# The last product of a gap in a pair of the maxima's PSUM banks, and the values in two halves: one change to an attention-and-experts block

## The chip, the cores and the metric

The kernel runs on one core of a Trainium2 chip. The metric is the device time of one execution in microseconds. The kernel before takes 2642.56 us, the median of three runs (2640.65 to 2642.76). The execution that the profiler recorded took 2650.03 us, and its trace spans 2648.3 us from the first to the last instruction.

## The reference

The input x has 32 sequences of 512 tokens with 256 features, in float32. Two causal attentions with 16 heads of 16 features follow each other. What the kernel calls a = 0 is ordinary attention with x itself as values; a = 1 has the same queries, other keys, and as values what the first attention got wrong.

```python
qk = x @ W_attn + b_attn                 # q and k
y  = causal_attn(q, k, v=x)
e  = x[:, 1:] - y[:, :-1]
k2 = x[:, :-1] @ W_k2 + b_k2
y2 = causal_attn(q[:, 1:], k2, e)        # one row of zeros ahead
x  = layernorm(x + proj(y) + proj(y2))
x  = layernorm(x + experts(x))           # 8 experts, top 2, summed by token
```

The experts' part has 512 tokens, those of the first sequence; for the 31 other sequences the second norm follows the first directly. Shapes and types of all results stay as they are in the kernel before.

## The kernel before, in words

**Groups and steps.** Four heads make a group, four groups a sequence, so there are 128 groups. `step(n)` (line 654) is called once for each n and works on several groups at once: the maxima of the scores of group n, the scores and exponentials of group n-1 (a = 0, and of n-2 for a = 1), the values of group n-2 and the normalization of n-2 and n-3.

**Slots and gaps.** A step has five slots (`slot`, line 393; the shapes are in `units`, line 263, and `banks`, line 345), and behind each slot a gap, filled from the list `rest[s]`. In a slot TensorE computes two things for a pair of heads at a time: the maxima's products (`sm`, lines 286 and 301), which VectorE reduces to a largest value per query (`top`, line 325), and the scores' products (`sc`, line 365), which ScalarE turns into exponentials (`pt`, line 382); GpSimd then cuts the diagonal block (line 386). Pair 1 of the scores comes first, then pair 0 of the maxima, then pair 1 of the maxima interleaved with pair 0 of the scores. In slots 0 and 3 each pair of maxima has two reductions, 768 and 256 columns wide; in the other slots it has one of 1024 columns.

**What fills the gaps.** In most steps: behind slot 0 the transposed maxima (`mt`, line 338) and then a half projection (`pj`, line 223, odd n) or an output projection (`po`, line 526, even n); behind slot 1 the values for a = 0 (`av`, line 434); behind slot 2 a transposition (`yt`, line 449) and a projection (`pj`); behind slot 3 `yt` and then `pj` or `po`; behind slot 4 the values for a = 1, in every fourth step with two transpositions `ys` (line 515) behind them. In the steps 12 to 20 the experts' products (`gu`, `dn`) stand ahead of these. A filling is one accumulation in one PSUM bank, and ScalarE or VectorE then copies it out. In `values` the four heads' products write four different strips of 32 partitions of one bank, four blocks of keys after each other, and one copy of 512 columns (line 442) takes them out.

**PSUM.** Its eight banks are in two pools. `bank` (line 79) hands out one bank of four: the scores' four products of a slot use them all, and so does every filling. `pair_of_banks` (line 76) hands out two neighbouring banks, and there are two such pairs: the maxima of a slot's pair 0 take one, those of pair 1 the other. A pool hands out what has been free longest, so the banks go round in turn, and a tile's first product waits until the last reader of the bank's previous tile is done.

**Order.** TensorE and SyncE run in the order of the code (`manual_schedule`, line 67); the order of the other engines is made by a scheduler. TensorE issues in order: a product that waits holds up those behind it.

Of the kernel before, what the change touches and what calls it, by code (L numbers as in the profile page):

```python
# [39 lines left out]
def block_kernel(  # L40
# [35 lines left out]
    def pair_of_banks(name):  # L76
        return psum.tile([P, NH2, T], F32, tag="two", name=name, bufs=2)

    def bank(name):
        return psum.tile([P, T], F32, tag="one", name=name, bufs=4)  # L80


# [246 lines left out]
    def halve(n):  # L329
        t, top = mx[n % 2], groups[n]["top"]  # L330
        nc.vector.tensor_copy(half(t[:, :, :, 0:2]), top)
        nc.vector.tensor_sub(half(t[:, :, :, 2:4]), top, t[:, :, :, 0:2])

    def augment(n):
        d = groups[n]
        ps = bank(f"mt{n}")
        for i in range(NB):
            nc.tensor.transpose(ps[:, i * P : (i + 1) * P], mx[n % 2][:, i].rearrange("p h s -> p (h s)"), ident)  # L338
        d["m"] = grp.tile([P, T], F32, tag="m", name=f"m{n}")
        nc.scalar.copy(half(d["m"]), ps)  # L340
# [82 lines left out]
            if after:  # L423
                after()

    def values(n, a):
        b, g = divmod(n, NG)
        d = groups[n]
        vals = (v_pad, e_pad)[a]
        ps = bank(f"av{n}_{a}")  # L430
        order = [0, 2, 1, 3] if a == 0 else [0, 1, 3, 2]
        for j in order:
            for h in range(GH):
                nc.tensor.matmul(  # L434
                    ps[HS * h : HS * (h + 1), j * P :],
                    vals[:, j, (g * GH + h) * HV : (g * GH + h) * HV + HS],
                    d["pt", a, j, h // NH2][:, h % NH2],
                    start=(j == order[0]),
                    stop=(j == order[-1]),
                )  # L440
        avs = d["avs", a] = work.tile([P, T], F32, tag="avs", name=f"avs{n}_{a}")
        nc.scalar.copy(avs, ps)  # L442

    def normalize(n, a):
        b, g = divmod(n, NG)
# [52 lines left out]
    def load_residual(b):  # L498
        s = seqs[b]
        s["xr"] = seq.tile([P, NB, C], F32, tag="xr", name=f"xr{b}", bufs=1)  # L500
        nc.sync.dma_start(s["xr"], x[b].rearrange("(n p) c -> p n c", p=P))

    def biased(b, part):

        two = slice(2 * part, 2 * part + 2)
        t = seqs[b]["xr"]
        nc.gpsimd.tensor_add(t[:, two], t[:, two], bp2.unsqueeze(1).to_broadcast([P, 2, C]))

    def turn(b):
        s = seqs[b]  # L510
        ysT = s["ysT"] = work.tile([P, NC, T], F32, tag="ysT", name=f"ysT{b}", bufs=1)
        for c in range(NC):
            ps = bank(f"ys{b}_{c}")
            for i in range(NB):
                nc.tensor.transpose(ps[:, i * P : (i + 1) * P], s["y"][:, i, c * P : (c + 1) * P], ident)  # L515
            nc.scalar.copy(ysT[:, c], ps)

    def attended(b, i):

# [50 lines left out]

        nc.vector.tensor_scalar(wt, wt, 0.5, None, ALU.mult)

    def biases():
        acc = moe["acc"] = seqs[0]["h"]
        for k in range(NB * C // T):
            ps = bank(f"bd{k}")
            for i in range(2 * k, 2 * k + 2):
                nc.tensor.matmul(
                    ps[:, (i % 2) * C : (i % 2 + 1) * C], moe["wT"][0:E, i * P : (i + 1) * P], moe["b_dn"],
                    start=True, stop=True,  # L580
                )
            two = slice(2 * k, 2 * k + 2)
            nc.vector.tensor_add(acc[:, two], ps.rearrange("p (i c) -> p i c", c=C), acc[:, two])

    def turn_tokens():
        moe["xT"] = const.tile([P, NC, T], F32, name="x1T")
        for c in range(NC):
            ps = bank(f"x1T{c}")
            for i in range(NB):
                nc.tensor.transpose(ps[:, i * P : (i + 1) * P], seqs[0]["h"][:, i, c * P : (c + 1) * P], ident)  # L590
            nc.vector.tensor_copy(moe["xT"][:, c], ps)

    def load_hidden(e):
        gu = moe["gu", e] = seq.tile([P, NC, 2, NF * P], F32, tag="gu", name=f"gu{e}", bufs=1)
# [27 lines left out]
            nc.vector.tensor_scalar(t, t, -LIMIT, 1.0, ALU.max, ALU.add)  # L622
            nc.gpsimd.tensor_mul(moe["h", e][:, f], moe["sig"], t)

    def down(e):
        for k in range(NB * C // T):
            ps = bank(f"dn{e}_{k}")
            for i in range(2 * k, 2 * k + 2):
                for f in range(NF):
                    nc.tensor.matmul(  # L630
                        ps[:, (i % 2) * C : (i % 2 + 1) * C],
                        moe["h", e][:, f, i * P : (i + 1) * P],
                        moe["dn", e][:, f],
                        start=(f == 0),
                        stop=(f == NF - 1),
                    )
            for i in range(2 * k, 2 * k + 2):
                nc.vector.scalar_tensor_tensor(
                    moe["acc"][:, i],
                    ps[:, (i % 2) * C : (i % 2 + 1) * C],  # L640
                    moe["w"][:, i, e : e + 1],
                    moe["acc"][:, i],
                    ALU.mult,
                    ALU.add,
                )

# [7 lines left out]
    def step(n):  # L654
        ready = lambda k: 0 <= k < n_all
        rest = [[] for _ in units]
        b, r = divmod(n, NG)
        if r == 1 and b + 1 < B:
            load(b + 1)
        if r == 3 and b + 1 < B:  # L660
            load_next(b + 1)
        if ready(n):
            prepare(n)
        if ready(n - 3):
            rest[3].append(lambda: normalize(n - 3, 1))
        if ready(n):
            rest[4].append(lambda: halve(n))
        if ready(n - 1):
            rest[0].append(lambda: augment(n - 1))
        if ready(n - 2):  # L670
            soon = n > n_all
            rest[0 if soon else 1].append(lambda: values(n - 2, 0))
            rest[1 if soon else 2].append(lambda: normalize(n - 2, 0))
            rest[4].append(lambda: values(n - 2, 1))
        two = n // 2 + 1
        if ready(2 * two):
            if n % 2 == 0:
                rest[2].append(lambda: project(two, 1))
                rest[4].append(lambda: spread(two, 1))
            else:  # L680
                rest[2] += [lambda: project(two, 0), lambda: spread(two, 0)]
                rest[0].append(lambda: project(two, 2, 0, T // 2))
                rest[3] += [lambda: project(two, 2, T // 2), lambda: spread(two, 2)]
        b, r = divmod(n - 3, NG)
        if r == NG - 1 and 0 <= b < B:
            rest[4].append(lambda b=b: turn(b))

        for b in range(B):
            end = (b + 1) * NG - 1
            last = b == B - 1  # L690
            for part in range(2):
                if n == (end + 4 if last else min(end + 5 + 2 * part, n_all)):
                    for i in range(2 * part, 2 * part + 2):
                        rest[0 if last or i % 2 == 0 else 3].append(lambda b=b, i=i: attended(b, i))
                if n == (end + 3 if last else end + 4):
                    rest[1 + 2 * part].append(lambda b=b, part=part: biased(b, part))
            if n == (end + 2 if last else end + 3):
                rest[3].append(lambda b=b: load_residual(b))
            if 0 < b < B - 1 and n == end + 8:
                rest[1].append(lambda b=b: store(b))  # L700


        e = n - first_expert
        if e == -1:
            rest[4] += [route, turn_tokens, lambda: load_hidden(0), lambda: load_down(0)]
        if e == 0:
            rest[0].insert(0, biases)
        if 0 <= e < E:
            rest[3].insert(0, lambda: hidden(e, 0, 0))
            rest[4].insert(0, lambda: hidden(e, 0, 1))  # L710
        if 0 <= e - 1 < E:
            rest[0].insert(0, lambda: hidden(e - 1, 1, 0))
            rest[1].insert(0, lambda: hidden(e - 1, 1, 1))
            rest[2].insert(0, lambda: down(e - 1))
            if e < E:
                rest[1].append(lambda: load_hidden(e))
                rest[2].append(lambda: load_down(e))
        if e == E:
            rest[4].append(lambda: second_norm(0, moe["acc"]))
        for s in range(len(units)):  # L720
            slot(n, s)
            for f in rest[s]:
                f()

    for m in range(3):
        project(0, m)
# [91 lines left out]
```

## Time and profile before

| | before |
|---|---|
| median of three runs | 2642.56 us (2640.65 to 2642.76) |
| the profiled execution | 2650.03 us |
| its span in the trace | 2648.3 us |
| mean granted TensorE clock | 0.989 |
| VectorE busy | 1943.7 us (73%) |
| ScalarE busy | 1757.0 us (66%) |
| GpSimd busy | 1724.0 us (65%) |
| TensorE matmul records | 33,808 |
| copies of the values, line 442 | 256 of 587 ns |

How to read it: busy is the time in which an engine executes at least one instruction. TensorE has two rows in the profile, PE for products and PEld for loads of the stationary operand. The ends of products are modelled, so the distance from one product's start to the next one's tells more than their durations. The 1.7 us between the profiled execution's time and its span lie before the first and after the last instruction. From slot 0 to the next step's slot 0 most steps of the trace take 19.1 us, and every fourth, that with the `ys`, 20.1 us.

### The profile page before, as it was taken

The numbers are of one execution on the slowest core, as the hardware profiler recorded it, in microseconds if no ns is written. First come the engines' busy times: TensorE is split into PE (matmuls) and PEld (weight loads), VectorE is DVE, ScalarE is ACT, GpSimd is POOL, SyncE is SP. The second block draws the span as 40 slices with busy tenths as digits, with TensorE's granted clock in tenths as the row PEclk, the third lists the DMA queues.
The fourth block names the chain that finished last, engine by engine and source line by source line (L and its number), as shares of the span: only waits on it lengthen the run. The fifth ranks groups of instructions, "written<-read, shape, count | busy, mean of one in ns | idle before, by whom it ended". The sixth has DMA issues, their size and how long they took to land.

```text
span 2648.3 us, 82677 instructions
## 1 busy us (share of the span) xinstructions
PE 2569.7 (97%) x33808; PEld 1742.7 (66%) x33808; DVE 1943.7 (73%) x3225; ACT 1757.0 (66%) x3416; POOL 1724.0 (65%) x3318
## 2 busy tenths in 40 slices
PE   6999999999999999999999999999999999999997
PEld 3666666666666666666666666666666666666665
DVE  5777777677777777777777777777777777777773
ACT  2666554467777767776767777676777767677774
POOL 4555555567666676766667666666766666676664
PEclk7999999999999999999999999999999999999998
DMA  5233233233334343333433333343333334233320
GB/s 136 69 89 89 73 85 91 79 81 97 89 75 104 83 104 82 95 90 74 105 81 99 88 91 93 75 105 81 90 96 90 94 76 104 82 90 96 88 67 25
DMA packets 167402, 231.91 MB, mean 88 GB/s; under 512 B 21624, under 2 KB 91248, under 8 KB 167024
## 3 DMA queue, kind: packets, MB, share of 16 engines
q1 hardware_dynamic: 164592, 226.17, 33.1%
q8 instruction: 269, 4.41, 0.7%
q14 instruction: 109, 0.89, 0.1%
q10 hardware_dynamic: 2368, 0.42, 0.1%
q0 software_dynamic: 64, 0.02, 0.0%
HBM read 75.41 MB, written 16.78 MB: 35 GB/s over the span
## 4 chain that ended last, share of the span: by engine, by line
PE 91%; ACT 3%; issue 2%; POOL 2%; DVE 2%; DMA 1%; SPq 0%; ACTq 0%; POOLq 0%; DVEq 0%
PE sc L365 28%; PE av L434 22%; PE pj L223 13%; PE sm L301 10%; PE yt L449 6%; PE po L526 4%; PE mt L338 3%; ACT pt L382 2%; PE gu L607 2%; PE ys L515 1%; PE dn L630 1%; DVE top L325 1%; PE sm L286 1%; POOL pk L241 0%; DMA bp_qk<-in_b_qkk 0%
## 5 line engine op out<-in xcount | busy, mean ns | idle before, releaser
L325 DVE TENSOR_REDUCE top<-sm 128x2 f32<-128x768 f32 (+3 forms) x1800 | 1536.3, 907 | 589.0 <-PE sc L365 328.7
L382 ACT ACTIVATE pt<-sc 128x512 f32<-128x512 f32 (+1 forms) x2564 | 1323.3, 602 | 322.9 <-PE sc L365 315.9
L386 POOL TENSOR_SCALAR_AFFINE_SELECT pt<-pt 128x256 f32<-128x256 f32 x2048 | 787.7, 407 | 531.1 <-ACT pt L382 530.3
L301 PE MATMUL sm<-kk_t,q_t 32*128 32x512 f32 (+2 forms) x7168 | 1034.8, 381 | 18.7 <-DVE top L325 9.0
L365 PE MATMUL sc<-q_t,kk_t 32*128 32x256 f32 (+3 forms) x8192 | 1045.5, 338 | 3.4 <-DVE h L529 2.0
L365 PEld LDWEIGHTS sc<-q_t,kk_t 32*128 32x128 f32 x8192 | 701.2, 184 | 260.4 <-issue 160.2
L365 PE MATMUL sc<-m,minus 32*128 32x256 f32 (+3 forms) x4096 | 756.4, 318 | 0.0
L301 PEld LDWEIGHTS sm<-kk_t,q_t 32*128 32x128 f32 x7168 | 613.8, 190 | 25.2 <-DVE top L325 11.7
L365 PEld LDWEIGHTS sc<-m,minus 32*128 32x128 f32 x4096 | 507.1, 185 | 10.0
L223 PE MATMUL pj<-xT,wq_sb 128*128 128x256 f32 (+1 forms) x1020 | 400.3, 516 | 8.5 <-DVE wq_sb L112 8.5
L442 ACT COPY avs<-av 128x512 f32<-128x512 f32 x256 | 150.2, 587 | 325.9 <-PE av L434 325.9
L286 PE MATMUL sm<-hide,pick 32*128 32x256 bf16 (+1 forms) x2560 | 339.2, 258 | 0.0
L434 PE MATMUL av<-pt,e_pad 128*32 128x512 f32 (+3 forms) x4096 | 304.2, 437 | 17.9 <-ACT pt L382 13.3
L434 PE MATMUL av<-pt,v_pad 128*32 128x512 f32 (+3 forms) x4096 | 304.4, 437 | 14.6 <-POOL pt L386 4.2
L235 ACT ACTIVATE pk<-pj,bp_qk 128x256 f32<-128x256 f32 (+1 forms) x255 | 151.2, 593 | 194.7 <-PE pj L223 185.4
L241 POOL TENSOR_TENSOR pk<-pk,lead 128x512 fp32r<-128x512 f32 x192 | 244.7, 1274 | 15.7 <-ACT lead L240 5.0
L434 PEld LDWEIGHTS av<-pt,v_pad 128*32 128x32 f32 x4096 | 136.8, 110 | 170.3 <-issue 128.4
L223 PEld LDWEIGHTS pj<-xT,wq_sb 128*128 128x128 f32 x1020 | 176.1, 192 | 96.1 <-issue 65.1
L434 PEld LDWEIGHTS av<-pt,e_pad 128*32 128x32 f32 x4096 | 130.9, 110 | 152.8 <-issue 148.0
L478 POOL TENSOR_TENSOR y<-y,y 128x256 f32<-128x256 f32 x128 | 96.4, 753 | 118.7 <-DVE mv L542 68.2
L449 PE MATMUL yt<-ident,avs 128*128 128x128 f32 x1024 | 168.0, 287 | 2.1 <-ACT pt L382 0.9
L449 PEld LDWEIGHTS yt<-ident,avs 128*128 128x128 f32 x1024 | 109.2, 141 | 75.3 <-ACT pt L382 70.3
(90 smaller groups left out, 1980.5 us busy)
## 6 DMA issues: line engine op xcount, KB each, us to landing
q_t<-lead SPq DMA_DIRECT2D x256, 128.0 KB
q_t<-pk SPq DMA_DIRECT2D x256, 128.0 KB
kk_t<-lead SPq DMA_DIRECT2D x256, 128.0 KB
kk_t<-pk SPq DMA_DIRECT2D x256, 128.0 KB
xT<-in_xT SPq DMA_DIRECT2D x32, 512.0 KB
x<-in_x SPq DMA_DIRECT2D x32, 512.0 KB
xr<-in_x SPq DMA_DIRECT2D x32, 512.0 KB
out<-h SPq DMA_DIRECT2D x31, 512.0 KB
```

The source lines that it names most:

```text
L223: nc.tensor.matmul(ps[:, 0 : hi - lo], wq_sb[:, m, c, part * P : (part + 1) * P], seqs[b]["xT"][:, c, lo:hi], start=(c == 0), stop=(c == N ...
L235: nc.scalar.activation(pk[:, lo:hi], ps[:, 0 : hi - lo], AF.Identity, bias=bp_qk[:, m, part : part + 1])
L241: nc.gpsimd.tensor_sub(half(pk), pk, lead)
L286: nc.tensor.matmul(ps[hh][:, 0 if alone else hh].rearrange("p (k c) -> p k c", c=P)[:, first::step], pick[rows], hide[rows, kinds[0] : kin ...
L301: nc.tensor.matmul(part(ps[hh], i, na, at)[:, 0 if alone else hh], half(d["q"][rows, k, i * P : (i + 1) * P]), half(d["kk"][rows, a : a + ...
L325: nc.vector.tensor_reduce(to, view, AX.X, ALU.max)
L365: nc.tensor.matmul(ps[hh][:, at * P : at * P + T - j * P], half(keys), half(queries[:, j * P :]), start=(k == 0), stop=(k == 2),)
L382: nc.scalar.activation(pt[:, hh, lo:hi], ps[hh][:, lo:hi], AF.Exp, scale=HD**-0.5)
L386: nc.gpsimd.affine_select(diag, diag, pattern=[[0, NH2], [1, P]], compare_op=ALU.is_ge, fill=0.0, base=-a, channel_multiplier=-1,)
L434: nc.tensor.matmul(ps[HS * h : HS * (h + 1), j * P :], vals[:, j, (g * GH + h) * HV : (g * GH + h) * HV + HS], d["pt", a, j, h // NH2][:, ...
L442: nc.scalar.copy(avs, ps)
L449: nc.tensor.transpose(ps[:, i * P : (i + 1) * P], d["avs", a][:, i * P : (i + 1) * P], ident)
```

## The change

A flag says that a filling is the last in its gap that uses a bank. While it is set, `bank` hands out the first bank of a pair from the maxima's pool in place of one of the four. So that every entry of a gap's list uses exactly one bank, functions that used several are called once for each: the values in two halves of 256 queries, `turn`, `biases`, `turn_tokens` and `down` once for each bank that they fill. The lists are written in another way but come out in the same order; an entry is now marked as one that fills a bank (`do`) or one that does not (`also`).

```diff
+    last_of_gap = [False]
+
     def bank(name):
+        if last_of_gap[0]:
+            return pair_of_banks(name)[:, 0]
         return psum.tile([P, T], F32, tag="one", name=name, bufs=4)
...
-    def values(n, a):
+    def values(n, a, lo, hi):
...
-        ps = bank(f"av{n}_{a}")
-        order = [0, 2, 1, 3] if a == 0 else [0, 1, 3, 2]
+        ps = bank(f"av{n}_{a}_{lo}")
+        order = [j for j in ([0, 2, 1, 3] if a == 0 else [0, 1, 3, 2]) if j * P < hi]
         for j in order:
+            at = max(lo, j * P)
             for h in range(GH):
                 nc.tensor.matmul(
-                    ps[HS * h : HS * (h + 1), j * P :],
+                    ps[HS * h : HS * (h + 1), at - lo : hi - lo],
                     vals[:, j, (g * GH + h) * HV : (g * GH + h) * HV + HS],
-                    d["pt", a, j, h // NH2][:, h % NH2],
+                    d["pt", a, j, h // NH2][:, h % NH2, at - j * P : hi - j * P],
...
-        avs = d["avs", a] = work.tile([P, T], F32, tag="avs", name=f"avs{n}_{a}")
-        nc.scalar.copy(avs, ps)
+        if lo == 0:
+            d["avs", a] = work.tile([P, T], F32, tag="avs", name=f"avs{n}_{a}")
+        nc.scalar.copy(d["avs", a][:, lo:hi], ps[:, 0 : hi - lo])
...
-            rest[0 if soon else 1].append(lambda: values(n - 2, 0))
-            rest[1 if soon else 2].append(lambda: normalize(n - 2, 0))
-            rest[4].append(lambda: values(n - 2, 1))
+            for lo, hi in ((0, T // 2), (T // 2, T)):
+                do(0 if soon else 1, values, n - 2, 0, lo, hi)
+            do(1 if soon else 2, normalize, n - 2, 0)
+            for lo, hi in ((0, T // 2), (T // 2, T)):
+                do(4, values, n - 2, 1, lo, hi)
...
         for s in range(len(units)):
             slot(n, s)
-            for f in rest[s]:
+            filling = [k for k, (_, fills) in enumerate(rest[s]) if fills]
+            for k, (f, _) in enumerate(rest[s]):
+                last_of_gap[0] = k == filling[-1] if filling else False
                 f()
+            last_of_gap[0] = False
```

In the built kernel the instructions of SyncE, VectorE and GpSimd are the same and in the same order as before. ScalarE has 256 copies more, each pair of half copies where the whole one stood. TensorE has the products in the same order, with the values' split: 24 in place of 16 for each of 256 values.

More of the change, by code (lines that the diff above doesn't have):

```diff
@@ L507, in biased, with turn @@
         nc.gpsimd.tensor_add(t[:, two], t[:, two], bp2.unsqueeze(1).to_broadcast([P, 2, C]))
-    def turn(b):
+    def turn(b, c):
         s = seqs[b]
[L511 to L516, printed above, removed]
+        if c == 0:
+            s["ysT"] = work.tile([P, NC, T], F32, tag="ysT", name=f"ysT{b}", bufs=1)
+        ps = bank(f"ys{b}_{c}")
+        for i in range(NB):
+            nc.tensor.transpose(ps[:, i * P : (i + 1) * P], s["y"][:, i, c * P : (c + 1) * P], ident)
+        nc.scalar.copy(s["ysT"][:, c], ps)
     def attended(b, i):
@@ L571, in route, with biases, turn_tokens @@
         nc.vector.tensor_scalar(wt, wt, 0.5, None, ALU.mult)
-    def biases():
+    def biases(k):
         acc = moe["acc"] = seqs[0]["h"]
[L575 to L591, printed above, removed]
+        ps = bank(f"bd{k}")
+        for i in range(2 * k, 2 * k + 2):
+            nc.tensor.matmul(
+                ps[:, (i % 2) * C : (i % 2 + 1) * C], moe["wT"][0:E, i * P : (i + 1) * P], moe["b_dn"],
+                start=True, stop=True,
+            )
+        two = slice(2 * k, 2 * k + 2)
+        nc.vector.tensor_add(acc[:, two], ps.rearrange("p (i c) -> p i c", c=C), acc[:, two])
+    def turn_tokens(c):
+        if c == 0:
+            moe["xT"] = const.tile([P, NC, T], F32, name="x1T")
+        ps = bank(f"x1T{c}")
+        for i in range(NB):
+            nc.tensor.transpose(ps[:, i * P : (i + 1) * P], seqs[0]["h"][:, i, c * P : (c + 1) * P], ident)
+        nc.vector.tensor_copy(moe["xT"][:, c], ps)
     def load_hidden(e):
@@ L623, in hidden, with down @@
             nc.gpsimd.tensor_mul(moe["h", e][:, f], moe["sig"], t)
[L625 to L639, printed above, removed]
+    def down(e, k):
+        ps = bank(f"dn{e}_{k}")
+        for i in range(2 * k, 2 * k + 2):
+            for f in range(NF):
+                nc.tensor.matmul(
                     ps[:, (i % 2) * C : (i % 2 + 1) * C],
[L641 to L644, printed above, removed]
-                )
+                    moe["h", e][:, f, i * P : (i + 1) * P],
+                    moe["dn", e][:, f],
+                    start=(f == 0),
+                    stop=(f == NF - 1),
+                )
+        for i in range(2 * k, 2 * k + 2):
+            nc.vector.scalar_tensor_tensor(
+                moe["acc"][:, i],
+                ps[:, (i % 2) * C : (i % 2 + 1) * C],
+                moe["w"][:, i, e : e + 1],
+                moe["acc"][:, i],
+                ALU.mult,
+                ALU.add,
+            )
     n_all = B * NG
@@ L663, in step @@
             prepare(n)
+        do = lambda gap, f, *args: rest[gap].append((partial(f, *args), True))
+        also = lambda gap, f, *args: rest[gap].append((partial(f, *args), False))
+        e = n - first_expert
+        if e == 0:
+            for k in range(NB * C // T):
+                do(0, biases, k)
+        if 0 <= e - 1 < E:
+            do(0, hidden, e - 1, 1, 0)
+            do(1, hidden, e - 1, 1, 1)
+            for k in range(NB * C // T):
+                do(2, down, e - 1, k)
+        if 0 <= e < E:
+            do(3, hidden, e, 0, 0)
+            do(4, hidden, e, 0, 1)
         if ready(n - 3):
-            rest[3].append(lambda: normalize(n - 3, 1))
+            do(3, normalize, n - 3, 1)
         if ready(n):
-            rest[4].append(lambda: halve(n))
+            also(4, halve, n)
         if ready(n - 1):
-            rest[0].append(lambda: augment(n - 1))
+            do(0, augment, n - 1)
         if ready(n - 2):
             soon = n > n_all
-            rest[0 if soon else 1].append(lambda: values(n - 2, 0))
-            rest[1 if soon else 2].append(lambda: normalize(n - 2, 0))
-            rest[4].append(lambda: values(n - 2, 1))
+            for lo, hi in ((0, T // 2), (T // 2, T)):
[3 more added lines that the diff above has]
+                do(4, values, n - 2, 1, lo, hi)
         two = n // 2 + 1
@@ L677, in step @@
             if n % 2 == 0:
-                rest[2].append(lambda: project(two, 1))
-                rest[4].append(lambda: spread(two, 1))
-            else:
-                rest[2] += [lambda: project(two, 0), lambda: spread(two, 0)]
-                rest[0].append(lambda: project(two, 2, 0, T // 2))
-                rest[3] += [lambda: project(two, 2, T // 2), lambda: spread(two, 2)]
+                do(2, project, two, 1)
+                also(4, spread, two, 1)
+            else:
+                do(2, project, two, 0)
+                also(2, spread, two, 0)
+                do(0, project, two, 2, 0, T // 2)
+                do(3, project, two, 2, T // 2)
+                also(3, spread, two, 2)
         b, r = divmod(n - 3, NG)
         if r == NG - 1 and 0 <= b < B:
-            rest[4].append(lambda b=b: turn(b))
+            for c in range(NC):
+                do(4, turn, b, c)
         for b in range(B):
@@ L693, in step @@
                     for i in range(2 * part, 2 * part + 2):
-                        rest[0 if last or i % 2 == 0 else 3].append(lambda b=b, i=i: attended(b, i))
+                        do(0 if last or i % 2 == 0 else 3, attended, b, i)
                 if n == (end + 3 if last else end + 4):
-                    rest[1 + 2 * part].append(lambda b=b, part=part: biased(b, part))
+                    also(1 + 2 * part, biased, b, part)
             if n == (end + 2 if last else end + 3):
-                rest[3].append(lambda b=b: load_residual(b))
+                also(3, load_residual, b)
             if 0 < b < B - 1 and n == end + 8:
-                rest[1].append(lambda b=b: store(b))
-        e = n - first_expert
+                also(1, store, b)
         if e == -1:
[L705 to L717, printed above, removed]
+            do(4, route)
+            for c in range(NC):
+                do(4, turn_tokens, c)
+            also(4, load_hidden, 0)
+            also(4, load_down, 0)
+        if 0 < e < E:
+            also(1, load_hidden, e)
+            also(2, load_down, e)
         if e == E:
-            rest[4].append(lambda: second_norm(0, moe["acc"]))
+            also(4, second_norm, 0, moe["acc"])
         for s in range(len(units)):
             slot(n, s)
-            for f in rest[s]:
+            filling = [k for k, (_, fills) in enumerate(rest[s]) if fills]
+            for k, (f, _) in enumerate(rest[s]):
+                last_of_gap[0] = k == filling[-1] if filling else False
                 f()
+            last_of_gap[0] = False
     for m in range(3):
```

## The prediction

> **What bounds the kernel now.** I read the page's first part, then its chain of work that ended last, then the list of waits, then the timeline around two gaps.
>
> ```profile
> PE 2569.7 (97%) x33808; PEld 1742.7 (66%) x33808; DVE 1943.7 (73%) x3225; ACT 1757.0 (66%) x3416; POOL 1724.0 (65%) x3318
> ...
> PE 91%; ACT 3%; issue 2%; POOL 2%; DVE 2%; DMA 1%; SPq 0%; ACTq 0%; POOLq 0%; DVEq 0%
> ```
>
> TensorE's own order sets the end: 91% of the chain are its products. Time is won or lost only where it starts something later than its own stream allows.
>
> ```profile
> PEld yt L449 <- ACT pt L382: 70.3, 245, 0.6
> ...
> PEld mt L338 <- ACT pt L382: 43.5, 124, 0.7
> ...
> PEld sm L301 <- DVE top L325: 11.7, 6, 4.8
> ```
>
> Engine, tile, line, then who was waited for, total us, times, longest. A gap's first filling (`yt`, `mt`) waits for the first exponential of the slot ahead, since that frees its bank. The maxima's pairs cost nearly nothing: six waits for VectorE in the whole run.
>
> Two gaps, from the timeline (start, duration in us). Step 61, slot 3 and the gap behind it:
>
> ```profile
> 1312.49 2.49 DVE L325 TENSOR_REDUCE top<-sm 128x2 f32<-128x768 f32 x4 [1.35 <-PE sc L365]
> ```
> ```profile
> 1313.14 0.66 PE L449 MATMUL yt<-ident,avs 128*128 128x128 f32 x4
> 1313.63 1.10 PE L223 MATMUL pj<-xT,wq_sb 128*128 128x256 f32 x4
> 1314.66 0.44 PE L365 MATMUL sc<-q_t,kk_t 32*128 32x384 f32 x2
> 1314.68 0.50 PE L301 MATMUL sm<-kk_t,q_t 32*128 32x512 f32 x2
> ```
>
> Step 62, slot 0 and its gap:
>
> ```profile
> 1319.96 2.48 DVE L325 TENSOR_REDUCE top<-sm 128x2 f32<-128x768 f32 x4 [0.95 <-PE sc L365]
> ```
> ```profile
> 1320.59 0.66 PE L338 MATMUL mt<-ident,mx 128*128 128x128 f32 x4
> 1321.08 1.12 PE L526 MATMUL po<-wp_sb,ysT 128*128 128x256 f32 x4
> 1322.13 0.44 PE L365 MATMUL sc<-q_t,kk_t 32*128 32x384 f32 x2
> 1322.15 0.49 PE L301 MATMUL sm<-kk_t,q_t 32*128 32x512 f32 x2
> ```
>
> The reader is to see that the reductions go on far into the gap. In step 61 the four run from 1312.49 to 1314.98: a 768-column one (mean 952 ns by the groups) and a 256-column one (414 ns) for pair 0, then the same for pair 1, with overlaps of 0.08. So pair 0's banks are free at 1313.78, **after** `pj` starts at 1313.63, and pair 1's at 1314.98, **after** the next slot's first maxima product at 1314.68. In step 62 pair 0 is free at 1321.25 against `po` at 1321.08, pair 1 at 1322.44 against 1322.15. Today none of this is felt, since `pj` and `po` take a scores' bank, and the next slot's pair 0 takes the banks freed first.
>
> **The change part by part.**
>
> *The last filling moves to a pair.* With two pairs in turn it gets the banks of the slot's pair 0, and the next slot's pair 0 gets those of pair 1, a turn later than today. The built kernel's order shows this, and that in these gaps the filling then waits on two semaphores (VectorE's and TensorE's own). What a wait costs beyond its cause: for one semaphore, the first exponential of 1312.46 ends 0.60 later, at 1313.06, and `yt` starts at 1313.14, so 0.08. For two, the `av` of the same step waits so already, and the chain gives
>
> ```profile
> 1315.85 0.61 ACT pt L382
> 1316.45 0.14 issue
> 1316.59 2.36 PE av L434 x32
> ```
>
> about 0.15 from the end of the exponential. I take 0.15, since that is the same form, and keep 0.08 as the lower end.
>
> - Behind slot 3: 1313.78 + 0.15 - 1313.63 = 0.30 us late. Read like this at each of the 114 gaps there with two fillings and no experts: mean 0.293, 33.4 us.
> - Behind slot 0: 1321.25 + 0.15 - 1321.08 = 0.32. 114 gaps, mean 0.324: 36.9 us.
> - The first steps have gaps with a single filling, which itself moves: twelve gaps, 9.2 us by the same reading.
> - Behind slot 2 the one 1219 ns reduction frees the pair in time (on average 2.13 us after the slot's start, `pj` starts at 2.24): nothing. Behind slot 1 also nothing: the second half starts 0.64 us after the first, at 2.53, the pair is free at 2.29.
> - Behind slot 4 VectorE is late with the normalization: 88 gaps, 0.18 each, 16.1 us as the trace stands. But slot 4 then starts 0.29 later, and VectorE's work ahead of it does not, save in the even steps, where it contains the `po` copy. I take 3 us.
>
> Steps 12 to 20 have a third filling in the gaps behind slots 0 and 3; their last starts a microsecond later and waits for nothing.
>
> *The next slot's maxima, pair 0.* They now wait for pair 1's reductions: 1315.13 against 1314.68, 0.45, of which the gap's delay already gives 0.30. The rest is 0.148 on average behind slot 3 and 0.121 behind slot 0, together 30.8 us. Behind the waiting product stands all else of the slot, since TensorE issues in order. But pair 1's scores were issued ahead, and the next gap's `av` waits for their exponential anyway (1316.44, when the slot's last products had ended at 1316.37), so part of the delay disappears there. I take half, 15.4 us, with 0 and 30.8 as ends. Pair 1 of the maxima waits for the last filling's copy; that ends ahead of need in all slots but 3, where the 512-column `pj` copy (687 ns) ends within 0.05 us of it: nothing.
>
> *What it takes away.* Today the second head of the scores' pair 0 waits for the last filling's copy and starts after the first: by 0.06 us on average behind the gap of slot 1, 0.14 behind 2, 0.11 behind 4. This goes behind 1 and 4. I give it nothing: the next gap's first filling waits for pair 1's exponential, which has ended 0.06 to 0.15 before it starts in each of these slots, so a slot that ends sooner only waits longer. Upper end: 0.06 x 118 + 0.11 x 117 = 20 us.
>
> *The values in halves.* Per value four heads x 6 products x 2 passes in place of 4 x 4 x 2: 4 more sets of four records, 1,024 sets in all. The columns stay 1280 a head and pass. Starts of today's sets, from the records: 512 columns every 428 ns, 384 every 321, 256 every 215, 128 every 109. That is 0.833 ns a column plus 2 ns a set: 1,024 x 2 ns = 2 us. The Trainium skill, "TensorEngine Tiling (Array Packing)", section Instruction Overhead, speaks against the split: each matmul carries about 60 cycles. Estimated from that page at 2.4 GHz (the figure of "TensorE: Matmul & The Clock Gate") that is 25 ns, 26 us for 1,024 sets, and the sum by it would be 24 us higher. The rows do not show such a charge down to 128 columns, the smallest used here, and decide.
>
> ScalarE makes two copies in place of one of 587 ns: by the nearest rows, a 272-column copy at 417 and a 256-column activation at 380, 0.17 to 0.25 us more, 44 to 63 us of its time. The first copy lies beside the second half's products, and the second is shorter than today's; ScalarE sat idle 325.9 us ahead of these copies. Without that cover it would cost up to 63 us. SyncE, GpSimd and VectorE keep their instructions in the same order, and no DMA moves.
>
> **The sum**, against the profiled execution: 36.9 + 33.4 + 9.2 + 15.4 + 3 + 2 = 99.9 us. That execution took 2650.0 us (span 2648.3), 7.5 above the median of the runs, 2642.6. The difference goes on the median: **2742.5 us**.
>
> **The rivals.**
>
> *Shorter waits (20%).* The price is 0.08, the pair 0 delay disappears wholly, and the scores' second head gains its 20 us: 114 x (0.254 + 0.223) = 54, + 8 for the single fillings, - 20: 42 us, 2685. For it: one-semaphore waits do take 0.08. Against: the two-semaphore form is in the built order.
>
> *All waits add up (10%).* Nothing of the 30.8 is absorbed and slot 4 keeps its 16 plus some 4 for its successor: 36.9 + 33.4 + 9.2 + 30.8 + 20 + 2 = 132, 2775. For it: TensorE is 97% busy, with little slack. Against: the `av` that waits for an exponential anyway.
>
> *The split binds (3%).* Each added set exposes its 110 ns weight load (line 434): 1,024 x 0.11 = 113 us more, 2855. Against: today's 128-column sets start every 109 ns with four such loads.
>
> *Faster (7%).* The late second head in the scores is what holds a slot, and freeing it shortens slots after the gaps of 1, 2 and 4 by all their lateness: 0.06 x 118 + 0.14 x 116 + 0.11 x 117 = 36 us, 2606, if the pairs come free in time. It decides from the point where the slot's reductions of pair 0 end 0.3 us sooner relative to the second filling than these rows say. Against: `mt` and `yt` follow the first exponential, not the slot's end.
>
> *No change (2%).* The new waits take the place of waits for exponentials, so that either the pairs are free or the loss is caught up.
>
> The forecast itself has 58%. From the first and second rivals' times and the forecast I make the range 2685 to 2775; 12% lie outside. Faster by over 0.2% (about what a measurement of this kernel can tell from no change) 7%, within 0.2% 2%, slower 91%.
>
> **What would show it.** In the new list of waits, `pj` and `po` behind VectorE's `top`, 228 times, some 0.3 us each, and the maxima (`sm`) too. In the timeline, `po` starts 0.15 after the second of four reductions. A step's length grows from 19.1 to about 19.8 us. `av` takes 2.37 in place of 2.36 us for both halves. I am wrong if `mt` or `yt` start sooner after a slot's start than 1.7 us, if the reductions in slots 0 and 3 start sooner than 1.1 us after it, or if `av` grows.

## The result, and the profile after

The changed kernel takes **2725.37 us** (median of four runs, 2723.3 to 2726.67), the kernel before 2642.4 us beside it: ratio 1.0315, 95% interval 1.0297 to 1.0332. It is 83 us slower; 99.9 were forecast on the same base, and 2725 lies in the range. The profiled execution took 2726.67 us with a span of 2725.0 us at a granted clock of 0.988, so the two profiled spans differ by 76.7 us. The working below is against that difference, since it can be followed step by step in the traces.

The first part of the page of after:

```profile
PE 2586.4 (95%) x37904; PEld 1847.2 (68%) x37904; DVE 1948.1 (71%) x3225; ACT 1783.9 (65%) x3672; POOL 1729.7 (63%) x3318
```

The reader is to see a span that is 77 us longer while no engine has much more to do: PE 17 us, ScalarE 27, VectorE and GpSimd 4 to 6. PE was busy in 97% of its span and is now in 95%. Only the row of weight loads grows by more, 105 us, with the split's 4,096 added loads; the split alone has them too (1852.5 us of loads) and takes 2647.9 us by its span. The loss is waiting, not work.

The list of waits of after (PEld for weight loads, PE for products; tile and line, who was waited for, total us, times, longest):

```profile
PEld yt L455 <- ACT pt L386: 80.9, 238, 0.7
...
PEld sm L305 <- ACT pk L239: 23.4, 125, 0.5
...
PEld pj L227 <- PE mt L342: 20.6, 55, 0.7
PEld po L532 <- PE mt L342: 20.3, 55, 0.4
...
PEld pj L227 <- PE yt L455: 15.3, 58, 0.3
...
PEld po L532 <- PE yt L455: 14.8, 56, 0.3
...
PE pj L227 <- DVE top L329: 12.6, 58, 2.0
...
PEld sm L305 <- DVE top L329: 9.7, 7, 3.9
...
PE po L532 <- DVE top L329: 8.8, 55, 0.2
```

The four rows of weight loads of `pj` and `po` are new: 71.0 us in 224 waits, 0.32 each. They are the late fillings behind slots 0 and 3. Two traps lie in this list. These rows name TensorE's own `mt` and `yt`, not VectorE's `top`: the filling waits on two semaphores, and the row puts the wait down to the wrong one, for in the timeline `mt` and `yt` are issued long before. The cause stands in the rows of the products, `pj` and `po` behind `top`, with 113 waits and 21.4 us; the line of `po` in step 62 below shows one of them. And the maxima that start late (`sm`) have no such row behind `top`: their load waits while a load of the scores still runs (from 1354.92 for 0.18 us in step 61, the late load starts at 1355.05), so this row shows no idle time. How late they are must be read from the timeline.

The same two gaps as before, from the timeline of after. Step 61, slot 3, VectorE and then TensorE:

```profile
1352.45 2.49 DVE L329 TENSOR_REDUCE top<-sm 128x2 f32<-128x768 f32 x4 [1.30 <-PE sc L369]
```
```profile
1353.18 0.66 PE L455 MATMUL yt<-ident,avs 128*128 128x128 f32 x4
1353.89 1.10 PE L227 MATMUL pj<-xT,wq_sb 128*128 128x256 f32 x4
1354.92 0.45 PE L369 MATMUL sc<-q_t,kk_t 32*128 32x384 f32 x2
1355.08 0.50 PE L305 MATMUL sm<-kk_t,q_t 32*128 32x512 f32 x2
```

Step 62, slot 0:

```profile
1360.26 2.48 DVE L329 TENSOR_REDUCE top<-sm 128x2 f32<-128x768 f32 x4 [1.25 <-PE sc L369]
```
```profile
1360.88 0.66 PE L342 MATMUL mt<-ident,mx 128*128 128x128 f32 x4
1361.69 1.10 PE L532 MATMUL po<-wp_sb,ysT 128*128 128x256 f32 x4 [0.16 <-DVE top L329]
1362.73 0.45 PE L369 MATMUL sc<-q_t,kk_t 32*128 32x384 f32 x2
1362.89 0.50 PE L305 MATMUL sm<-kk_t,q_t 32*128 32x512 f32 x2
```

The second of the four reductions ends 1.29 us after the first one's start, as before: at 1353.74 and 1361.55. `pj` follows 0.15 later and `po` 0.14. Before, `po` stood 0.49 behind `mt`; now it is 0.81. The fourth reduction ends at 1354.94 and 1362.74, and the next slot's first maxima product follows 0.14 and 0.15 behind it, in place of 0.02 behind the scores.

From slot to slot, medians of the steps 21, 25 and so on to 121 (a slot's length runs from its first product to the next slot's first). These steps have no `ys`. The steps 23, 27 and so on, the other odd ones, differ in slot 1 alone, which is 0.09 to 0.10 shorter in both kernels:

| | before | after |
|---|---|---|
| first filling after the start of slot 0, 2, 3 | 1.71, 1.75, 1.74 | 1.71, 1.74, 1.81 |
| last filling behind slots 0 and 3 | 2.20, 2.23 | 2.52, 2.52 |
| first `av` behind slots 1 and 4 | 1.92, 1.93 | 1.93, 1.95 |
| first weight load of the last filling, behind slots 0, 2, 3 | 2.196, 2.232, 2.196 | 2.494, 2.181, 2.493 |
| length of slot 0 | 3.26 | 3.56 |
| of slot 1 | 4.21 | 4.23 |
| of slot 2 | 4.15 | 4.10 |
| of slot 3 | 3.26 | 3.56 |
| of slot 4 | 4.22 | 4.25 |
| a step | 19.09 | 19.69 |

The row of weight loads tells more than that of the products: it moves by 0.30, -0.05 and 0.30, and so do the lengths of slots 0, 2 and 3.

### The profile page after: what moved, and what is told of

It is laid out like the page before. It is cut to its first block, busy times and chain, and to the rows that moved or that the text cites. A ratio compares the mean times of both kernels' runs of the same rounds, so it can differ in the third digit from the quotient of the medians.

```text
span 2725.0 us, 91382 instructions
## 1 busy us (share of the span) xinstructions
PE 2586.4 (95%) x37904; PEld 1847.2 (68%) x37904; DVE 1948.1 (71%) x3225; ACT 1783.9 (65%) x3672; POOL 1729.7 (63%) x3318
## 5 line engine op out<-in xcount | busy, mean ns | idle before, releaser
L369 PE MATMUL sc<-q_t,kk_t 32*128 32x256 f32 (+3 forms) x8192 | 1003.0, 333 | 1.0 <-DVE top L329 0.8
L369 PEld LDWEIGHTS sc<-q_t,kk_t 32*128 32x128 f32 x8192 | 640.3, 184 | 252.8 <-issue 204.6
L369 PE MATMUL sc<-m,minus 32*128 32x256 f32 (+3 forms) x4096 | 672.3, 318 | 0.0
L305 PEld LDWEIGHTS sm<-kk_t,q_t 32*128 32x128 f32 x7168 | 623.7, 190 | 56.0 <-ACT pk L239 23.4
L369 PEld LDWEIGHTS sc<-m,minus 32*128 32x128 f32 x4096 | 408.5, 184 | 9.9
L448 ACT COPY avs<-av 128x256 f32<-128x256 f32 x512 | 198.3, 387 | 252.7 <-PE av L439 252.7
L439 PE MATMUL av<-pt,v_pad 128*32 128x256 f32 (+1 forms) x6144 | 309.0, 349 | 14.4 <-POOL pt L390 3.9
L439 PE MATMUL av<-pt,e_pad 128*32 128x256 f32 (+1 forms) x6144 | 303.7, 345 | 16.2 <-DVE top L329 0.8
L439 PEld LDWEIGHTS av<-pt,v_pad 128*32 128x32 f32 x6144 | 204.3, 111 | 108.1 <-issue 27.0
L439 PEld LDWEIGHTS av<-pt,e_pad 128*32 128x32 f32 x6144 | 196.5, 109 | 84.9 <-issue 30.0
L455 PE MATMUL yt<-ident,avs 128*128 128x128 f32 x1024 | 167.0, 285 | 23.2 <-ACT pt L386 19.8
L242 POOL CAST lead<-pk 128x512 fp32r<-128x512 f32 x189 | 122.6, 649 | 76.9 <-ACT pk L239 76.9
```

Source lines behind the costliest of these rows:

```text
L305: nc.tensor.matmul(part(ps[hh], i, na, at)[:, 0 if alone else hh], half(d["q"][rows, k, i * P : (i + 1) * P]), half(d["kk"][rows, a : a + ...
L369: nc.tensor.matmul(ps[hh][:, at * P : at * P + T - j * P], half(keys), half(queries[:, j * P :]), start=(k == 0), stop=(k == 2),)
L439: nc.tensor.matmul(ps[HS * h : HS * (h + 1), at - lo : hi - lo], vals[:, j, (g * GH + h) * HV : (g * GH + h) * HV + HS], d["pt", a, j, h / ...
L448: nc.scalar.copy(d["avs", a][:, lo:hi], ps[:, 0 : hi - lo])
L455: nc.tensor.transpose(ps[:, i * P : (i + 1) * P], d["avs", a][:, i * P : (i + 1) * P], ident)
```

## The experiments

Theory: the loss is the wait of the last filling behind slots 0 and 3 for the slot's own late reductions. Rivals: the split of the values costs it (copies, weight loads, more products); or the maxima that wait a turn longer do. Each ratio is against the kernel before on the same chip, and a loss or gain in us is worked out from the ratio where no medians are given.

**The split alone.** The flag is never set, so no filling uses a pair.

```diff
-                last_of_gap[0] = k == filling[-1] if filling else False
+                last_of_gap[0] = False
```

> The changed kernel with the flag never set: every filling in one of the four scores' banks, the values still in two halves. Theory (the pairs come free too late, because VectorE's reductions in slots 0 and 3 run into the gap): the split is nearly free, 2 us for 1,024 more sets of products, so 2640 to 2648 us against 2642.4 before, and in the trace the second filling behind slots 0 and 3 starts 2.2 us after the slot's start as before. Rival (the split itself, its additional products, weight loads and copies, costs the time): near the changed kernel's 2725 us, 2700 or more.

Measured: ratio 1.0013 (1.0004 to 1.0022), 3.4 us (1.1 to 5.8), for 1,024 more sets of products, where 2 us had been forecast. The split is not the cause. It also shows a gain that comes to nothing: slots 0 and 2 now end 0.16 sooner, slot 0 in three steps of four (1.62 and 1.57 us after their start, before 1.78 and 1.74), as the second head of the scores is no longer held up by one copy of 512 columns. The first filling still starts at 1.71 and 1.75, behind the exponential.

The Trainium skill, "TensorEngine Tiling (Array Packing)", section Instruction Overhead, gives some 60 cycles a matmul; an estimate from it was 26 us for these sets. The 3.4 us measured are an eighth of that, so the rows were the better guide here.

**The pairs only behind slots 0 and 3**, with the values whole.

```diff
-                last_of_gap[0] = k == filling[-1] if filling else False
+                last_of_gap[0] = k == filling[-1] if filling and s in (0, 3) else False
...
-            for lo, hi in ((0, T // 2), (T // 2, T)):
-                do(4, values, n - 2, 1, lo, hi)
+            do(4, values, n - 2, 1, 0, T)
```

> The values whole as before; the last filling takes a pair behind slots 0 and 3 alone. Theory (late reductions): nearly all of the loss is here, 2 x 0.30 us in each of some 114 steps = 68 us, and 7 to 15 us from the maxima's wait in the next slot and the first steps' single fillings, so 2715 to 2728 us. Rival (the split, or the pairs behind slots 1, 2 and 4): under 2660 us.

Measured: ratio 1.0287 (1.0266 to 1.0307), 2717.95 us. Its steps grow by 0.63, its last fillings behind slots 0 and 3 start at 2.53, and the maxima of slots 1 and 4 start 0.16 after the slot, before 0.02. Two of the five gaps carry nearly all of the loss.

**The pairs everywhere but behind slots 0 and 3**, with the values in halves.

```diff
-                last_of_gap[0] = k == filling[-1] if filling else False
+                last_of_gap[0] = k == filling[-1] if filling and s not in (0, 3) else False
```

> The changed kernel, values in halves, with a pair for the last filling behind slots 1, 2 and 4 alone. Theory (late reductions): the pairs are free in time there; the projection behind slot 2 ends 0.05 us sooner, slot 3 ends 0.07 us later since its maxima wait for the projection's copy, the values take 0.01 us longer each: +0.04 us in each of 116 steps, 2643 to 2652 us. Rival (the split costs): 2700 or more. Rival (freeing the scores from the last filling's copy is worth time once the late pairs are out of it, up to 36 us): 2606 to 2638 us, faster than both.

Measured: 2659.94 us, ratio 1.0051 (1.0038 to 1.0065), 13.5 us, more than expected. The list of its waits has a row that after has only once:

```profile
PEld av L439 <- DVE top L329: 20.3, 86, 1.3
```

and the weight loads in the timeline, step 61, behind slot 4:

```profile
1319.18 0.62 PEld L439 LDWEIGHTS av<-pt,e_pad 128*32 128x32 f32 x16 [0.33 <-issue]
1320.01 1.24 PEld L439 LDWEIGHTS av<-pt,e_pad 128*32 128x32 f32 x32 [0.21 <-DVE top L329]
```

The second half of the values waits for the wide reduction of the slot's pair 0. This is the wait that the prediction read from the trace of before (88 gaps, 0.18 each) and set aside, since in after slot 4 starts later. Here slot 4 is not late, and the wait is back. In slot 3 the maxima's pair 1 also waits for the copy of `pj`, which moves `yt` from 1.74 to 1.81; in after that was covered, since the last filling waits longer anyway. In the steps of the table slot 4 grows by 0.15 and slot 2 shrinks by 0.05. From step 21 to step 124 the trace loses 7.1 us; where the rest of the 13.5 lies is not shown. So "faster" fails even without the two bad gaps: the second head of the scores does start sooner, and no step gets shorter by it.

**The pairs everywhere, the values whole.**

> The changed kernel with the values whole, so that a gap with the values alone puts all of them in a pair. Theory (late reductions): then the values wait for pair 0's reductions behind slots 1 and 4 too: they start 1.9 us after the slot's start now, the pair is free at 2.1 to 2.4 behind slot 1 and at 2.3 to 2.5 behind slot 4 (0.15 more for the two waits), so 0.4 to 0.7 us later in each, on top of the loss of the changed kernel: 2820 to 2880 us. Rival (the split costs the time and the pairs do not): under 2700 us.

Measured: 2829.1 us, ratio 1.069 (1.0676 to 1.0705). Behind slot 1 the only filling is `av`, and it takes the pair, so it starts 2.33 to 2.52 us after the slot's start in place of 1.82 to 1.92; behind slot 4, without the `ys`, 2.43 to 2.66 in place of 1.93. Splitting the values is what lets their gaps take a pair: the first half covers the reduction.

**Shorter reductions in slots 0 and 3**, with the change.

```diff
+                if u in (0, 3):
+                    view = view[..., 0 : view.shape[-1] // 2]
```

> The changed kernel with the reductions of slots 0 and 3 over half of their keys, so that some maxima are too small. By the rows of the profile (550 ns for a reduction of 384 columns, 280 for one of 128) pair 0 is then free 1.84 us after the slot's start and pair 1 at 2.6, ahead of the second filling at 2.2 and of the next slot's maxima at 3.27. Theory (late reductions): the waits behind slots 0 and 3 go, and so does the loss, but the wait behind slot 4 comes back as in the run without pairs behind 0 and 3: 2650 to 2662 us. Rival (it is the taking of a pair as such, its longer list of waits, not the lateness): 2700 or more.

**The same in the kernel before, as control.**

> The control to the run before it: the kernel before with the same shorter reductions. Theory: nothing waits for these reductions there, so within 0.2% of 2642 us. If it is faster by tens of us, shorter reductions help in themselves and the run before it says less.

Measured: 2664.68 us, ratio 1.0061 (1.0043 to 1.0079), with the change; 2674.18 us, ratio 1.0092 (1.007 to 1.0113), without. The control was to change nothing and lost 24 us: with shorter reductions the scheduler put VectorE's addition that empties `po`'s bank behind two other operations in even steps, and slot 4 waited for it. In the control the scores' second head did (it starts 1.58 us after the slot's start in step 64), with the change the maxima's pair 1 (1.57 in place of 0.91). Against this control the change has no cost left, but a control that moves is a poor one.

**Shorter reductions in odd steps only**, a pair of kernels in which VectorE's order stays as it was (GpSimd's moves a little, in both alike).

```diff
+                if u in (0, 3) and n % 2:
+                    view = view[..., 0 : view.shape[-1] // 2]
```

> The changed kernel, with the reductions of slots 0 and 3 made over half of the keys in odd steps only (maxima of half of the keys in those steps, so another result). If what the change costs is the wait of the last filling for the two late reductions: odd steps lose their .6 us and come out about .1 us shorter than the steps of the kernel before, even steps keep their .6; about 62 odd steps get back .7 us each, so some 40 us over the kernel before, ratio 1.013 to 1.018. If the cost lies elsewhere in the change: ratio 1.028 or more.

> Control: the kernel before with the same shorter reductions in odd steps only (again maxima of half of the keys there). No filling waits for them in this kernel, and VectorE's order stays: within .3% of the kernel before, ratio .997 to 1.003. If the shorter reductions help by themselves, it is faster by as much as the one with the change seems to gain.

Measured: with the change 2683.38 us, ratio 1.0131 (1.0114 to 1.0148); the control 2648.63 us, ratio 0.9997 (0.9988 to 1.0007). Odd steps (those of the table) take 18.97 us with the change and 19.09 in the control, even steps without `ys` 19.69 and 19.09. Of the four new rows of weight loads only these are left in this kernel:

```profile
PEld po L534 <- PE mt L344: 20.4, 55, 0.4
...
PEld po L534 <- PE yt L457: 15.0, 56, 0.3
```

`po` belongs to even steps, `pj` behind these slots to odd ones, and its rows are gone. Its timeline has an odd and an even gap behind slot 0:

```profile
1318.11 0.66 PE L344 MATMUL mt<-ident,mx 128*128 128x128 f32 x4
1318.60 1.03 PE L227 MATMUL pj<-xT,wq_sb 128*128 128x256 f32 x4
1319.56 0.44 PE L371 MATMUL sc<-q_t,kk_t 32*128 32x384 f32 x2
```
```profile
1337.09 0.66 PE L344 MATMUL mt<-ident,mx 128*128 128x128 f32 x4
1337.91 1.10 PE L534 MATMUL po<-wp_sb,ysT 128*128 128x256 f32 x4 [0.16 <-DVE top L331]
1338.94 0.44 PE L371 MATMUL sc<-q_t,kk_t 32*128 32x384 f32 x2
```

With the reductions out of the way `pj` stands 0.49 behind `mt`, as it did before the change, and the next slot follows 0.96 later (1.06 in the kernel before, by the medians of slot 0). That odd steps are even 0.12 shorter than in the control fits the weight loads: behind slot 0 the first one starts at 2.09 in place of 2.20, now that the bank is free (pair 0's reductions end at 1.84) before the second exponential is done (2.14). One kernel holds both cases side by side, and the late reductions are the cause.

**Only pair 1's reductions shorter**, with the change: the last filling still waits, the next slot's maxima do not.

```diff
+                if u in (0, 3) and pair == 1:
+                    view = view[..., 0 : view.shape[-1] // 2]
```

> The changed kernel with shorter reductions for pair 1 alone in slots 0 and 3, half of the keys. The second filling still waits for pair 0 as before, but the next slot's maxima of pair 0 no longer wait for pair 1 (free at 3.05 us after the slot's start, needed at 3.58). It prices that wait by itself, which the prediction put at 15.4 us, half of 30.8. If all of it holds the path: 30 us less than the changed kernel, ratio 1.020 to before. If the next gap's wait for an exponential swallows it, as the changed kernel's trace suggests (values start 1.93 us after the slot's start, against 1.91): 4 to 8 us less, ratio 1.028 to 1.030.

Measured: 2728.52 us, ratio 1.0301 (1.0283 to 1.0319). The maxima no longer wait (0.01 behind the scores), and a step takes 19.66 us in place of 19.69. In even steps VectorE's order moved again, so only odd ones are read. The second wait costs 0.02 to 0.03 us a step, some 3 us in all: the `av` behind it waits for its exponential in any case and starts at 1.91 in place of 1.93.

**What the pairs are good for.** Behind slot 2 the pair is free in time. In this version of the kernel before, the projection behind slot 2 is made in two halves of 256, the first half in a pair.

```diff
-                rest[2].append(lambda: project(two, 1))
+                rest[2].append(lambda: project(two, 1, 0, T // 2, True))
+                rest[2].append(lambda: project(two, 1, T // 2))
```

> The kernel before with one edit: behind slot 2, the only gap whose pair is free in time, the projection goes in two halves of 256 tokens, the first into a pair, the second into a scores' bank. Theory: the first half no longer waits for the second exponential (0.05 us), the maxima wait for the first half's copy, which is early, and the scores' second head for the second half's, which is shorter, so slot 3 ends up to 0.07 us sooner, of which the next exponential leaves 0.02: 0.07 us in each of 116 steps, 8 us, 2632 to 2638 us, faster than both kernels. Rival (exponentials hold every gap anyway): within 2 us of 2642.

Measured: **2640.41 us**, before 2646.45, ratio 0.9971 (0.9961 to 0.9982), a little faster than the kernel before. The same with both halves in the scores' banks:

> The kernel before with the projection behind slot 2 in two halves, both in the scores' banks, none in a pair. If the 8 us of the version with the first half in a pair came from the shorter last copy alone, this gains them too: ratio .996 to .998. If the pair is what gives them, because the first half need not wait for the second exponential's bank, the gain goes: the second half then waits for a later exponential's bank, ratio .999 to 1.005.

Measured: 2639.2 us, before 2646.63, ratio 0.9976 (0.9966 to 0.9985). The runs alone would put the gain down to the shorter last copy and not to the pair. The steady steps say the opposite: from step 21 to step 124 the version with the pair needs 1993.4 us, that without 1998.0, the kernel before 1999.5. The two versions differ in the bank of the first half alone. With the pair its weight load starts 2.18 us after slot 2's start, without it at 2.23, as in the kernel before, and slot 2 takes 4.11 us against 4.16 and 4.15. The shorter copy does what was expected of it in both: in slot 3 the scores' second head starts with the first (0.71 us after the slot's start, before 0.85), and `yt` follows at 1.71 in place of 1.74. But slot 3 gains nothing from that: it takes 3.26 us in all three, since the next filling's load still starts at 2.19 to 2.20, behind the second exponential (2.14).

So what these steps gain comes from the pair. The profiled spans of the version without it and of the kernel before differ by 12.3 us: 1.4 lie in these steps, 3.4 behind them and 7.4 ahead of them, where its granted clock was higher (0.80 in the first 50 us and 1.00 in the next, against 0.74 and 0.92 before). Over its ten runs the mean clock was 0.992, against 0.990. How much of the 7.4 us between the medians of the runs is the edit and how much the clock stays open.

## Why the prediction was right, and where it was off

The mechanism, its two places and the sign were right: that the second of four reductions ends after the last filling wants its bank was read from the trace of before, and the odd steps with shorter reductions show it. The total was 23 us too large against the profiled spans (17 against the medians). Term by term, in the profiled executions (each measured entry is a median times the prediction's count):

| term | put at | measured | from |
|---|---|---|---|
| last filling behind slots 0 and 3 | 70.3 | 68.4 | 114 x (0.30 + 0.30), lengths of the slots |
| single fillings of the first steps | 9.2 | 8.5 | first 12 steps +15.7, less 12 x 0.60 |
| next slot's maxima, pair 0 | 15.4 | 3.4 | 114 x 0.03, pair 1's reductions shorter |
| behind slot 4 | 3 | 0 | length of slot 4: +0.03, explained by the rows above and below |
| the split | 2 | 2.3 | 114 x (0.01 + 0.01), split alone; 3.4 by its runs |
| behind slot 2 | 0 | -5.8 | 116 x -0.05, length of slot 2 |
| sum | 99.9 | 76.8 | the spans differ by 76.7 |

That the sum meets the spans to 0.1 us is luck. By the starts of the steps, after is 15.7 us behind when step 12 begins, loses 1.1 in the steps 12 to 20, where the experts' products stand, 59.6 in the steps 21 to 123, 0.58 a step on average, and 0.2 after them.

- *Behind slots 0 and 3*: right to 0.02 us a gap. The price of 0.15 for a wait on two semaphores held: 0.14 and 0.15 above. So the rival "shorter waits" with 0.08 falls. Slot 0 grew by 0.30 where its filling moved by 0.32, since the prediction went by the first product and the slot by its weight load, which moved by 0.30: the first two products of a late filling are 0.29 us apart, before 0.31.
- *The first steps*: the least certain row. From the first maxima product to the start of step 2 it took 29.0 to 33.8 us in the seven kernels whose fillings behind slots 0 and 3 keep the scores' banks, and 36.1 in after, so half of this row could be what the start of an execution varies by.
- *The maxima of pair 0* is **the term that failed**: I took half of 30.8 us, and nearly all of it is absorbed, 3.4 is left. My own ground for halving, the `av` that waits for its exponential anyway, holds in nearly all of these gaps and not in half. That exponential ends 1.77 and 1.79 us after the starts of slots 1 and 4 before, 1.78 and 1.80 after, and `av` follows 0.15 later in both kernels. The delayed products of the slot end at 1.82 (modelled), still ahead of it. "All waits add up" falls by the same number.
- *Behind slot 2* I gave nothing and missed a gain of 0.05 a step. The whole `pj` still starts at 2.24, but its second product follows 0.48 us after its first, before 0.53. Its bank used to wait for the second exponential, which ends at 2.18; a pair is free earlier, at 2.13. So its first weight load runs ahead, at 2.18 in place of 2.23. The two versions with the halved projection, which differ in this bank alone, show the same 0.05.
- *Pair 1 of the maxima in slot 3* I called nothing because the `pj` copy ends within 0.05 of need. The list has it as 23.4 us in 125 waits. In after it is covered by the longer wait behind it; with the pairs only outside slots 0 and 3 it was seen.
- *Behind slot 4* the small number was right for the reason given: with slot 4 on time the wait came back, at 86 gaps of 0.24, where the trace of before had been read as 88 of 0.18.
- *The scores' second head* was right: it starts sooner (0.71 in place of 0.77 and 0.82) and the slots end sooner, yet no filling does. The rival "faster" falls with it.
- *What would show it*: the step went to 19.69 instead of 19.8, and `av` takes 2.37 us as said. The list of waits names `top` 113 times instead of 228, in the rows of the products, and `mt` and `yt` in those of the loads. The sign "reductions sooner than 1.1 us" was set too close to tell anything: they start at 1.09 in both kernels.

Of the 23 us the failed term accounts for 12, slot 2 for 6, slot 4 for 3 and the late fillings for 2.

## What to carry to other kernels

Before a tile is moved to another pool of banks, read for each place where it stands when the last reader of that pool's banks ends, against when the tile's first weight load starts today; a pool whose reader is an engine that runs far into the gap is not free there, however few waits it shows now. Then read whether the next thing on the engine waits for something else anyway: that decides if a second delay adds up, and here the answer was nearly all or nothing for each place rather than half. A bank that is free sooner is worth what the filling's first weight load gains by it, here 0.05 us a step behind slot 2, and half as wide a last copy without such a bank left the steady steps as long as they were.

## What the runs showed of the hardware

- The instruction that waits on two semaphores starts 0.14 to 0.15 us after the later one's cause (the `pj` and `po` above), one that waits on a single semaphore 0.05 to 0.08 (the second half of `av` behind slot 4, with the pairs only outside slots 0 and 3: its load and first product start at 1320.01, the reduction of 1318.74 with 1.21 us ends at 1319.95; the prediction's `yt` is the 0.08).
- What a filling's lateness costs is read from its first weight load: with 256 columns the second product starts 0.32 us after that load, whether the load starts 2.09 us after slot 0 (odd steps with shorter reductions), 2.20 (before) or 2.49 (after). Behind slot 3 the first product starts at 2.23 before and at 2.31 in those odd steps, but both loads start at 2.20, and slot 3 takes 3.26 in both.
- The same kernel's time moves with the granted clock of the whole run: among the runs of the kernel before, those at a mean clock of 0.987 took 2651.1 to 2654.8 us, those at 0.993 took 2640.4 to 2642.4. Differences of 2 to 3 us between kernels are as well read from the steady steps as from a few runs.
- Less work can cost time: halving the reductions of slots 0 and 3 in all steps let the scheduler move one addition on VectorE, and the kernel before lost 24 us by it; halving them in odd steps moved nothing on VectorE, and its time stayed (ratio 0.9997).
